# A due time for each single operation: a list scheduler's keys in a fused attention and recurrence kernel

## The chip, the cores and the metric

The kernel runs on one core of one Trainium2 chip. The metric is the device time of one execution in microseconds (us); the time before is the median of three runs. The core has five engines that each work through their own queue in order: PE (matmul), DVE (vector), ACT (scalar functions), POOL (general) and SP, which here only starts transfers. In the profile, PEld is the loading of weights into PE.

## The reference, cut to what matters

The input is x of 2 batches, 2048 rows, 256 features. A layer of gated linear attention with 16 heads comes first: each score of query t and key s is multiplied by a decay (from a running sum of gates) and by a weight that depends on the level of t XOR s. Then follow an output projection and two layer norms, a short gated recurrence over the two batches, and a last layer norm.

```python
Q = (x @ Wq.T); K = (x @ Wk.T); V = (x @ Wv.T); dl = (x @ Wdl.T)
g = -exp(A_log) * softplus(x @ Wdt.T + dt_bias);  cg = cumsum(g, axis=1)
Lam = softplus(Lp * dl)
W = (Q K^T) * S**-0.5 * exp(cg_t - cg_s) [s <= t] * Lam[t, level(t, s)]
x = layernorm(x + layernorm_g_b((W V) @ Wout.T + x))
# recurrence over the two batches, at each of the 2048 rows:
c = sigmoid(x wf + c uf + bf) * c + sigmoid(x wi + c ui + bi) * tanh(x wc + c uc + bc)
h = tanh(x wo + c_final uo + bo)
x = layernorm(x + h)
```

## The kernel before, in words

The 2048 rows are cut into 16 chunks of 128. Within a chunk, scores are computed in full; over chunks, four running states (N0 to N3, one for each bit of the chunk's number) carry the sums that later chunks need. Most matmuls are split into two half-precision parts, a high one and a low one (names ending in h and l), so that each product is three matmuls.

For every chunk, `body` calls `project` (tile pv: values and gate inputs; z, m, u, ln: softplus; pc: running sum; RP, pt, RT: rows that go to memory and come back as R and st), `keys` (pqk, with F and L as its two parts), `attend` (pu, pS: the new state; arg and DL: exponentials; sc: scores; pi: the sum over values; pin: the part from the states; YT) and `finish` (po, layer norms, gt and tg: gates, pcu, ph, hh, out). In chunk 0, the weights wo and fw are also loaded, by nine transfers through a ring of two x1 buffers, and pg (a small product with the initial state of the recurrence) is computed from them.

None of these calls starts an instruction. `Engine` and `Recorder.add` record 3845 operations; an operation is one instruction, or a group of matmuls that is kept together (918 groups stand for 10382 matmuls). `depend` finds which operation needs which. `order` then makes the final order of each engine's queue, with a small simulation: an engine that is free takes, of the operations whose inputs are ready and whose buffers are free, the one with the lowest key `late`. `issue` writes the instructions out in that order, all at one line of the code (L536 in the profile), so views by line tell nothing here and views by tile do.

The keys before: `DUE` has one due time for each chunk's output. `late` is carried back from there over the dependences (an operation must be done a duration and a latency ahead of its earliest user). Then `BIAS`, one number for each kind of operation (engine and tile, with own numbers for the first, the last and the last but one chunk: @0, @9, @8), is added. `FIRST` sets the order of the first sixteen transfers by hand. `STICK` would make PE prefer its present mode (matmuls over 128 rows, over 64 rows, or into 32 columns); it is negative, so `max(..., 0)` leaves it without effect.

`BUFS` gives the number of buffers of each ring; a ring's tiles are taken in the order in which they were recorded. `BANKS` caps how many of the eight banks that PE writes to each class of tile may hold: y (pv, pc, pt, pqk), z (po, pt_x, gt, pcu, ph), x (pu, pS, pin), a (arg), s (sc), p (pi), t (gates of the last chunk).

Of the kernel before, what the change touches and what calls it, by code (L numbers as in the profile page):

```python
# [22 lines left out]
P = 128  # L23
B, T, D = 2, 2048, 256
# [8 lines left out]
DUE = [  # L33
    2677.57, 7721.13, 18978.35, 19716.23, 26604.1, 27450.81, 30772.73, 32390.67,
    34188.43, 36425.9, 37687.87, 40156.28, 43733.31, 46896.49, 47598.73, 59076.43,
]
BIAS = {
    'DVE:id16': -544.41, 'POOL:mhalf': -2585.45, 'POOL:ones': -884.87, 'POOL:RP': 1536.59, 'DMA:xt32@0': -4046.65,
    'DVE:xth@0': 1406.88, 'POOL:xtl@0': -518.54, 'DMA:xn@0': -2368.1, 'DMA:LpB@0': -3281.08, 'POOL:LpB@0': 860.85,
    'DVE:LpB@0': -244.97, 'DMA:bc_dtb@0': -2440.29, 'DMA:stg_wv@0': -6352.72, 'ACT:wv_h@0': -1203.55,  # L40
    'DVE:wv_l@0': 268.05, 'DMA:bc_Alog@0': -6629.31, 'ACT:bc_Alog@0': -1742.76, 'DVE:bc_Alog@0': -856.29,
    'DMA:mk@0': -4013.56, 'DMA:tri@0': -3595.99, 'DMA:stg_wq@0': -3921.89, 'ACT:wq_h@0': -1587.01,
    'DVE:wq_l@0': 1004.73, 'DMA:stg_wk@0': -4796.3, 'ACT:wk_h@0': 1541.09, 'DVE:wk_l@0': 3050.85,
    'DMA:st@0': -6284.79, 'DMA:R0@0': -6277.05, 'DMA:R1@0': -5991.07, 'POOL:SH@0': 665.45, 'POOL:SL@0': -2142.9,
    'POOL:VZ0@0': 1168.73, 'POOL:VZ1@0': -2626.46, 'PE:pv@0': -2541.05, 'DVE:z@0': -3273.44, 'ACT:VZ0@0': -4024.21,
    'POOL:z@0': -405.5, 'DVE:m@0': 572.33, 'ACT:u@0': 300.83, 'ACT:ln@0': 419.02, 'DVE:u@0': -1545.81,
    'ACT:LL@0': -482.21, 'POOL:g@0': -945.72, 'POOL:gp@0': 847.34, 'POOL:gr@0': 2525.08, 'PE:pc@0': -832.96,
    'POOL:LL@0': -1927.28, 'POOL:lf@0': -892.19, 'DVE:RP@0': 1443.6, 'DVE:r1@0': -759.26, 'PE:pt@0': -4539.93,
    'ACT:RT@0': -4433.14, 'DMA:scr@0': -628.34, 'DMA:cg2@0': -2529.67, 'POOL:E@0': -1904.15, 'ACT:E@0': -1974.72,
    'POOL:wv@0': 181.98, 'PE:pqk@0': 64.39, 'ACT:F@0': 1604.82, 'DVE:L@0': 240.14, 'DMA:bc_lng@0': 2134.89,  # L50
    'DMA:bc_lnb@0': -3284.28, 'DMA:bc_bo@0': 2756.69, 'DMA:ic@0': 2678.73, 'DMA:fb@0': 1506.14,
    'DMA:stg_wo@0': 214.04, 'ACT:wo_h@0': 749.49, 'DVE:wo_l@0': 13.57, 'DMA:stg_fw@0': 1917.56,
    'ACT:fw_h@0': -4483.73, 'DVE:fw_l@0': 3214.87, 'DVE:ich@0': 420.52, 'DVE:icl@0': -4538.93, 'PE:pg@0': 1562.45,
    'DVE:gb@0': 1718.11, 'PE:pu@0': 476.98, 'ACT:Uh@0': 2949.46, 'DVE:Ul@0': 1151.14, 'PE:pS@0': 1579.04,
    'ACT:N0@0': -3364.34, 'POOL:Ne0@0': -1812.42, 'POOL:Nt0@0': 2666.57, 'PE:arg@0': 1940.26, 'ACT:DL@0': 617.53,
    'PE:sc@0': 1032.21, 'DVE:DL@0': -2154.89, 'PE:pi@0': 14.24, 'ACT:YT@0': -2007.66, 'DVE:YTl@0': -1029.9,
    'ACT:SH@0': -122.62, 'DMA:xc@0': -943.46, 'PE:po@0': 1994.93, 'DVE:o@0': 25.16, 'POOL:xc@0': 1259.58,
    'DVE:st6@0': -1858.28, 'DVE:mv@0': -3427.79, 'POOL:rs@0': -1949.61, 'DVE:x1@0': -5553.71, 'PE:pt_x@0': -1400.7,
    'ACT:tr_x@0': -2328.9, 'DVE:tr_x@0': 2309.54, 'PE:gt@0': -1288.93, 'ACT:tg@0': -946.21, 'DVE:ct@0': -235.27,
    'DVE:c20@0': -3271.11, 'ACT:chh@0': -1127.08, 'DVE:chl@0': 554.25, 'DVE:c21@0': -872.21, 'PE:pcu@0': 3059.02,  # L60
    'DVE:cu@0': 1460.37, 'PE:ph@0': 1875.67, 'DVE:hh@0': -3488.44, 'ACT:hh@0': 132.07, 'POOL:hh@0': 3054.19,
    'DMA:out@0': 3049.1, 'DMA:xt32': -1810.23, 'DVE:xth': 64.72, 'POOL:xtl': -114.25, 'DMA:xn': -34.41,
    'PE:pv': -827.63, 'DVE:z': -1783.61, 'ACT:VZ1': -2672.79, 'POOL:z': 778.86, 'DVE:m': -789.82, 'ACT:u': 160.38,
    'ACT:ln': 591.53, 'DVE:u': 565.39, 'ACT:LL': 4374.65, 'POOL:g': 743.3, 'POOL:gp': -706.56, 'POOL:gr': 1663.66,
    'PE:pc': -2010.17, 'POOL:LL': 2926.67, 'POOL:lf': 3821.96, 'DVE:RP': -662.55, 'DVE:r1': -2759.89,
    'PE:pt': -165.69, 'ACT:RT': 659.27, 'DMA:scr': -1065.41, 'DMA:cg2': -986.92, 'DMA:st': 2349.73,
    'DMA:R0': -4459.06, 'DMA:R1': -920.98, 'POOL:E': 164.31, 'ACT:E': 3751.96, 'POOL:wv': -2316.25,
    'PE:pqk': 3231.38, 'ACT:F': 2373.65, 'DVE:L': 1459.54, 'POOL:ca': 2673.82, 'ACT:coef': 777.82,
    'PE:pu': 1486.59, 'ACT:Uh': -1034.21, 'DVE:Ul': -1341.83, 'PE:pS': -1300.83, 'ACT:N1': -1363.27,
    'POOL:Ne1': 3295.45, 'POOL:Nt1': -3412.65, 'POOL:mt': -860.48, 'POOL:N1': 1496.08, 'PE:arg': 10.51,  # L70
    'ACT:DL': -378.27, 'PE:sc': 1271.55, 'DVE:DL': 214.57, 'PE:pi': -1471.85, 'PE:pin': 557.54, 'DVE:Yi': 2234.51,
    'ACT:Yh': 1604.54, 'POOL:Yl': 569.07, 'ACT:YT': -714.54, 'DVE:YTl': -122.31, 'ACT:SH': 3886.77,
    'POOL:SL': -2249.79, 'DMA:xc': 1825.76, 'PE:po': -3323.98, 'DVE:o': -660.15, 'POOL:xc': -169.22,
    'DVE:st6': -348.25, 'DVE:mv': -2225.59, 'POOL:rs': 414.73, 'DVE:x1': -228.81, 'PE:pt_x': -545.23,
    'ACT:tr_x': -194.42, 'DVE:tr_x': 94.93, 'PE:gt': -1722.42, 'ACT:tg': -1182.38, 'DVE:ct': -4965.5,
    'DVE:c20': -807.68, 'ACT:chh': -2859.38, 'DVE:chl': -3393.25, 'DVE:c21': 92.69, 'PE:pcu': -3235.88,
    'DVE:cu': 958.49, 'PE:ph': 1685.23, 'DVE:hh': -2322.3, 'ACT:hh': -1393.34, 'POOL:hh': 1020.15,
    'DMA:out': -1687.37, 'ACT:VZ0': 887.84, 'ACT:N0': -1579.9, 'POOL:Ne0': 662.46, 'POOL:Nt0': 2273.86,
    'POOL:acc0': 1222.8, 'ACT:N2': 2274.54, 'POOL:Ne2': -1305.11, 'POOL:Nt2': 3789.98, 'POOL:N2': -2988.84,
    'DVE:tq': -1338.55, 'POOL:Yi': -418.52, 'POOL:acc1': -4347.71, 'ACT:N3': -1472.76, 'POOL:Ne3': -1671.15,  # L80
    'POOL:Nt3': -1206.59, 'POOL:N3': 747.56, 'DMA:xc@8': 15056.81, 'PE:po@8': 11984.32, 'DVE:o@8': 12872.18,
    'POOL:xc@8': 12701.25, 'DVE:st6@8': 9516.16, 'DVE:mv@8': 11273.9, 'POOL:rs@8': 13415.76, 'DVE:x1@8': 7496.93,
    'PE:pt_x@8': 12669.14, 'ACT:tr_x@8': 11859.29, 'DVE:tr_x@8': 8427.28, 'PE:gt@8': 10079.09,
    'ACT:tg@8': 16255.28, 'DVE:ct@8': 13065.88, 'DVE:c20@8': 12123.56, 'ACT:chh@8': 6769.1, 'DVE:chl@8': 13861.4,
    'DVE:c21@8': 9374.46, 'PE:pcu@8': 9104.07, 'DVE:cu@8': 14670.33, 'PE:ph@8': 10197.25, 'DVE:hh@8': 14713.5,
    'ACT:hh@8': 13013.82, 'POOL:hh@8': 17906.53, 'DMA:out@8': 8066.82, 'DMA:xt32@9': -3472.99,
    'DVE:xth@9': -6943.2, 'POOL:xtl@9': -7979.66, 'PE:pv@9': -7250.49, 'DVE:z@9': -7399.69, 'ACT:VZ1@9': -5093.65,
    'POOL:z@9': -8444.59, 'DVE:m@9': -3821.67, 'ACT:u@9': -8298.34, 'ACT:ln@9': -7589.28, 'DVE:u@9': -8544.13,
    'ACT:LL@9': -4666.75, 'POOL:g@9': -6445.41, 'POOL:gp@9': -525.04, 'POOL:gr@9': 1071.48, 'PE:pc@9': -5094.17,
    'POOL:LL@9': -7512.85, 'POOL:lf@9': -7085.42, 'DVE:RP@9': -8900.61, 'DVE:r1@9': -5745.08, 'PE:pt@9': -6171.97,  # L90
    'ACT:RT@9': -9289.92, 'DMA:scr@9': -5138.62, 'DMA:cg2@9': -12451.75, 'DMA:st@9': -8335.6, 'DMA:R0@9': -4913.0,
    'DMA:R1@9': -1320.23, 'PE:pqk@9': -5086.21, 'ACT:F@9': -2346.26, 'DVE:L@9': -4425.52, 'POOL:ca@9': -1966.77,
    'POOL:acc0@9': -4203.44, 'POOL:acc1@9': -2628.34, 'POOL:acc2@9': -6977.55, 'ACT:coef@9': -5726.39,
    'PE:arg@9': -8364.73, 'ACT:DL@9': -6371.85, 'PE:sc@9': -2442.58, 'DVE:DL@9': -5936.8, 'PE:pi@9': -8104.24,
    'PE:pin@9': -6842.43, 'DVE:Yi@9': -7958.54, 'DVE:tq@9': -4871.42, 'POOL:Yi@9': -9414.91, 'ACT:Yh@9': 923.7,
    'DVE:Yl@9': -13.59, 'ACT:YT@9': -5899.02, 'DVE:YTl@9': 948.32, 'DMA:xc@9': -3131.16, 'PE:po@9': -10407.06,
    'DVE:o@9': -6391.56, 'POOL:xc@9': -5874.17, 'PE:warm@9': 2241.77, 'DVE:st6@9': -3233.97, 'DVE:mv@9': -6158.55,
    'POOL:rs@9': -4272.53, 'DVE:x1@9': -8481.89, 'PE:pt_x@9': -10891.67, 'ACT:tr_x@9': -8747.79,
    'DVE:tr_x@9': -3011.58, 'DVE:b16@9': -459.04, 'PE:ph1@9': 2189.17, 'PE:gt0@9': -1044.0, 'ACT:tg@9': -4313.81,
    'DVE:ct@9': -4064.32, 'DVE:c20@9': -8811.46, 'ACT:chh@9': -9398.28, 'DVE:chl@9': -4364.2, 'PE:gt1@9': -8791.8,  # L100
# [1027 lines left out]
```

## Time and profile before

| what | value |
|---|---|
| median of 3 runs | 614.29 us (613.6 to 614.72) |
| the profiled execution, its own time | 615.93 us |
| its span, first to last instruction | 614.1 us |
| mean granted TensorE clock | 0.991 |
| PE busy | 585.6 us, 95% |
| weight loads busy | 504.2 us, 82% |
| DVE busy | 502.4 us, 82% |
| ACT busy | 383.4 us, 62% |
| POOL busy | 303.5 us, 49% |
| transfers | 46.36 MB, mean 75 GB/s |

The profiled execution is 1.64 us longer than the median; 1.8 us of its time lie around the span. A matmul's record lasts longer than the time until the next one starts, since matmuls are pipelined: busy time on PE is the union of such records. Where this text speaks of a pitch, it means the time from one matmul's start to the next one's start.

### The profile page before, as it was taken

To read this page: it belongs to the slowest core of one execution; us is meant where nothing else is said; L and a number is where in the kernel's file an instruction comes from. 1 tells how busy PE (TensorE), PEld (TensorE's weight loads), DVE (VectorE), ACT (ScalarE), POOL (GpSimd) and SP (SyncE) were. 2 spreads that over 40 slices of the span, in tenths; PEclk is the share of its full clock that TensorE was granted. 3 is DMA by queue.
4 is the path that set the end of the run, shared out by engine and by line. 5 is a ranking of instruction groups with operands and counts; after the bars stand their busy time and mean duration, and the time that the engine had idled before them with its cause. 6 is when DMAs were issued, how large, how long until landed. Compare 5 with 4: busy or idle time off the path is not lost.

```text
span 614.1 us, 24206 instructions
## 1 busy us (share of the span) xinstructions
PE 585.6 (95%) x10382; PEld 504.2 (82%) x10382; DVE 502.4 (82%) x1196; ACT 383.4 (62%) x914; POOL 303.5 (49%) x666
## 2 busy tenths in 40 slices
PE   5988999999999999999999999999999999999894
PEld 2776788988898788978889888888988889888794
DVE  5977958888879997789786888897978879787974
ACT  4666587465784856558664674857467594664552
POOL 4461646134735729244772464547376455353432
PEclk9998999999999999999999999999999999999997
DMA  8785134311243205041411514114050512203001
GB/s 245 182 189 130 36 73 91 90 35 38 60 101 91 71 3 141 20 108 35 110 36 37 125 37 91 54 25 119 20 141 21 108 37 75 70 4 101 27 2 35
DMA packets 70139, 46.36 MB, mean 75 GB/s; under 512 B 23984, under 2 KB 67760, under 8 KB 70000
## 3 DMA queue, kind: packets, MB, share of 16 engines
q1 hardware_dynamic: 70032, 44.82, 29.3%
q8 instruction: 81, 1.33, 0.9%
q14 instruction: 26, 0.21, 0.1%
HBM read 35.63 MB, written 9.18 MB: 73 GB/s over the span
## 4 chain that ended last, share of the span: by engine, by line
PE 45%; DVE 23%; POOL 13%; ACT 9%; DMA 6%; issue 3%; SPq 0%; POOLq 0%; ACTq 0%; DVEq 0%
PE gt L536 10%; PE pqk L536 9%; PE pi L536 4%; PE sc L536 4%; POOL rs L536 3%; DVE DL L536 3%; PE ph L536 3%; DVE L L536 3%; ACT DL L536 3%; DVE m L536 3%; PE pv L536 3%; PE arg L536 2%; PE pin L536 2%; DVE st L536 2%; PE pu L536 2%
## 5 line engine op out<-in xcount | busy, mean ns | idle before, releaser
L536 PEld LDWEIGHTS <-fw_h 128*128 128x128 f16 x1176 | 90.9, 98 | 5.0 <-ACT fw_h L536 2.0
L536 ACT ACTIVATE F<-pqk 128x512 f16<-128x512 f32 x128 | 73.7, 616 | 30.3 <-PE pqk L536 28.5
L536 DVE SCALAR_TENSOR_TENSOR L<-pqk,F 128x512 f16<-128x512 f32 x128 | 82.6, 676 | 5.9 <-ACT F L536 5.9
L536 DVE SCALAR_TENSOR_TENSOR DL<-sc,DL 128x512 f32<-128x512 f32 x128 | 81.7, 677 | 4.8 <-PE sc L536 3.6
L536 PE MATMUL gt<-tr_x,fw_h 128*128 128x128 f16 x768 | 82.6, 219 | 0.3 <-DVE tr_x L536 0.2
L536 PEld LDWEIGHTS <-wk_h 128*128 128x128 f16 x992 | 69.9, 98 | 6.2 <-issue 0.6
L536 ACT ACTIVATE tg<-gt,gb 128x128 f32<-128x128 f32 x192 | 53.8, 373 | 33.9 <-PE gt L536 33.3
L536 ACT ACTIVATE DL<-arg 128x512 f32<-128x512 f32 x128 | 68.1, 616 | 6.8 <-PE arg L536 6.5
L536 PE MATMUL pqk<-xth,wq_h 128*128 128x256 f16 x256 | 70.1, 274 | 0.3 <-DVE o L536 0.3
L536 PE MATMUL gt<-tr_x,fw_l 128*128 128x128 f16 x384 | 70.0, 219 | 0.0
L536 PE MATMUL pqk<-xtl,wq_h 128*128 128x256 f16 x256 | 70.0, 273 | 0.0
L536 PE MATMUL pqk<-xth,wq_l 128*128 128x256 f16 x256 | 69.9, 273 | 0.0
L536 PEld LDWEIGHTS <-F 64*128 64x128 f16 x2048 | 60.8, 93 | 10.9 <-issue 8.4
L536 PE MATMUL pqk<-xth,wk_l 128*128 128x256 f16 x256 | 69.8, 272 | 0.0
L536 PE MATMUL pqk<-xth,wk_h 128*128 128x256 f16 x256 | 69.8, 272 | 0.0
L536 PE MATMUL pqk<-xtl,wk_h 128*128 128x256 f16 x256 | 69.7, 272 | 0.0
L536 PEld LDWEIGHTS <-fw_l 128*128 128x128 f16 x588 | 57.3, 98 | 1.8 <-DVE fw_l L536 1.0
L536 PEld LDWEIGHTS <-wq_h 128*128 128x128 f16 x512 | 48.6, 98 | 8.0 <-issue 0.7
L536 POOL TENSOR_TENSOR Yi<-Yi,tq 128x256 f32<-128x256 f32 x32 | 25.3, 791 | 49.2 <-DVE Yi L536 33.3
L536 PEld LDWEIGHTS <-wk_l 128*128 128x128 f16 x496 | 46.2, 98 | 4.1 <-issue 1.0
L536 PE MATMUL sc<-F 64*128 64x128 f16 x512 | 46.4, 218 | 0.3 <-DVE L L536 0.3
L536 PEld LDWEIGHTS <-L 64*128 64x128 f16 x1024 | 45.2, 93 | 0.7 <-issue 0.4
(179 smaller groups left out, 1809.7 us busy)
## 6 DMA issues: line engine op xcount, KB each, us to landing
st<-cg SPq DMA_DIRECT2D x16, 768.0 KB, 6.3
xt<-xT SPq DMA_DIRECT2D x16, 256.0 KB, 2.8
xc<-x SPq DMA_DIRECT2D x16, 256.0 KB, 2.8
scr<-RT SPq DMA_DIRECT2D x16, 256.0 KB, 2.9
R<-scr SPq DMA_DIRECT2D x32, 128.0 KB, 2.9
xn<-x SPq DMA_DIRECT2D x15, 256.0 KB, 3.2
out<-hh SPq DMA_DIRECT2D x15, 256.0 KB, 2.2
stg_fw<-fw SPq DMA_DIRECT2D x8, 256.0 KB, 3.7
```

The costliest lines, as they stand in the source:

```text
L536: getattr(eng.real, meth)(*[real(x) for x in a], **{q: real(x) for q, x in k.items()})
```

## The change

The keys of all 3845 operations now stand in one table, two characters for each operation, in the order of recording. `DIGITS` are 89 printable characters; the number of a pair is read in base 89, and 200 is taken away. `order` no longer carries due times back over the dependences, and `DUE`, `BIAS`, `FIRST` with its field `rank`, and the term with `STICK` are gone. The ring sizes `BUFS` and the caps `BANKS` have other values. What is computed, the recorded operations, their dependences, the model of durations and latencies, and the rule by which a free engine chooses are as before.

```diff
-DUE = [
-    2677.57, 7721.13, 18978.35, 19716.23, 26604.1, 27450.81, 30772.73, 32390.67,
...
-BIAS = {
-    'DVE:id16': -544.41, 'POOL:mhalf': -2585.45, 'POOL:ones': -884.87, 'POOL:RP': 1536.59, 'DMA:xt32@0': -4046.65,
...
+DIGITS = "".join(chr(c) for c in range(33, 127) if chr(c) not in "\"\\'{}")
+PLAN = (
+    "_A#+Y4#U#y$)#d$NSU$3#x$2$G$/3g,/$-<YFn$x&C$3&uR5$2R^,[%D$2-U$,Zs$*%dFy0w$*$4$)$,$$!y$/]W$(E`JzOWZq#t$4,T0K!&#y+~"
...
+BUFS = {
+    'xt32': 1, 'xth': 2, 'xtl': 2, 'xn': 1, 'L': 3, 'F': 3, 'z': 1, 'm': 2, 'u': 2, 'ln': 1, 'LL': 1, 'g': 8,
+    'gp': 1, 'gr': 8, 'lf': 3, 'r1': 1, 'RT': 1, 'scr': 2, 'cg2': 2, 'E': 1, 'wv': 1, 'x1': 2, 'Uh': 2, 'Ul': 3,
+    'DL': 2, 'YT': 2, 'YTl': 4, 'xc': 1, 'o': 1, 'st6': 3, 'mv': 3, 'rs': 2, 'tr_x': 3, 'tg': 1, 'ct': 4, 'c20': 2,
+    'chh': 6, 'chl': 3, 'c21': 1, 'cu': 1, 'hh': 2, 'ca': 1, 'coef': 3, 'mt': 1, 'Yi': 5, 'Yh': 1, 'Yl': 5,
+    'acc0': 3, 'tq': 1, 'acc1': 1, 'acc2': 1, 'st69': 4, 'mv9': 2, 'rs9': 3,
 }
-BUFS = {
-    'xt32': 1, 'xth': 2, 'xtl': 2, 'xn': 1, 'L': 3, 'F': 3, 'z': 1, 'm': 1, 'u': 1, 'ln': 3, 'LL': 1, 'g': 3,
-    'gp': 10, 'gr': 3, 'lf': 4, 'r1': 1, 'RT': 1, 'scr': 2, 'cg2': 3, 'E': 1, 'wv': 1, 'x1': 2, 'Uh': 1, 'Ul': 5,
-    'DL': 2, 'YT': 4, 'YTl': 3, 'xc': 1, 'o': 1, 'st6': 4, 'mv': 4, 'rs': 3, 'tr_x': 2, 'tg': 1, 'ct': 1, 'c20': 1,
-    'chh': 2, 'chl': 6, 'c21': 1, 'cu': 4, 'hh': 2, 'ca': 3, 'coef': 2, 'mt': 1, 'Yi': 2, 'Yh': 1, 'Yl': 1,
-    'acc0': 5, 'tq': 1, 'acc1': 1, 'acc2': 1, 'st69': 7, 'mv9': 5, 'rs9': 2,
-}
-BANKS = {'y': 8, 'z': 8, 'x': 4, 'a': 7, 's': 5, 'p': 6, 't': 7,}
-
-FIRST = ["xt32", "stg_wv", "stg_wq", "LpB", "bc_dtb", "stg_wk", "bc_Alog", "tri", "mk", "xt32", "stg_wq", "stg_wk", "st", "R0", "R1", "xn"]
+BANKS = {'y': 6, 'z': 6, 'x': 8, 'a': 6, 's': 6, 'p': 8, 't': 3,}
 MERGE, WARM, TABLE, MODE = 0.6, 0.37, 1.28, 0.1
...
-    def order(self, outs):
+    def order(self, code):
...
-        late = [1e9] * n
-        for i in range(n - 1, -1, -1):
-            late[i] = min([outs.get(i, 1e9)] + [late[s] - ops[i].dur - ops[i].lat for s in succ[i]])
-        bias = BIAS
-        late = [x + bias.get(o.kind, bias.get(o.kind.split("@")[0], 0.0)) for x, o in zip(late, ops)]
-        late = [o.rank - 1e6 if o.rank >= 0 else x for x, o in zip(late, ops)]
-        stick = max(bias.get("STICK", 0.0), 0.0)
+        base = len(DIGITS)
+        late = [DIGITS.index(code[2 * i]) * base + DIGITS.index(code[2 * i + 1]) - 200 for i in range(n)]
...
-                    m = min((k for k in range(3) if ready[e][k]), key=lambda k: ready[e][k][0][0] + (stick if e == "PE" and k != mode else 0))
+                    m = min((k for k in range(3) if ready[e][k]), key=lambda k: ready[e][k][0][0])
```

## The prediction

> **What bounds the kernel now.** I read the page first, then the busy time by stretches, then what PE waited for, then the chain of waits, and last the transfers' queue at the start. The page, and PE's waits:
>
> ```profile
> span 614.1 us, 24206 instructions
> PE 585.6 (95%) x10382; PEld 504.2 (82%) x10382; DVE 502.4 (82%) x1196; ACT 383.4 (62%) x914; POOL 303.5 (49%) x666
> ...
> PE pv L536 <- DVE xth L536: 5.9, 1, 5.9
> PE arg L536 <- DVE L L536: 2.3, 6, 0.8
> PE pg L536 <- ACT fw_h L536: 1.8, 1, 1.8
> PE ph L536 <- ACT chh L536: 1.6, 1, 1.6
> PE pv L536 <- POOL xtl L536: 1.6, 1, 1.6
> ```
>
> PE is the bound. The waits are in us in total, times, longest: the first and the fifth are the head of the kernel, the fourth is its tail, and all others together come to about 12 us. The stretches show where PE idles (length, then busy us of PE, PEld, DVE, ACT, POOL, then the granted clock):
>
> ```profile
> 40.00:60.00 20.00, 15.61 (x291) 11.66 (x293) 13.25 (x28) 10.43 (x26) 7.23 (x16) 0.91 0.71 158
> 100.00:200.00 100.00, 99.83 (x1797) 86.82 (x1795) 84.54 (x207) 61.51 (x150) 44.71 (x92) 1.00 0.30 73
> 200.00:300.00 100.00, 97.58 (x1788) 84.21 (x1786) 87.88 (x207) 66.00 (x156) 52.16 (x116) 1.00 0.28 71
> 560.00:580.00 20.00, 18.04 (x408) 15.03 (x408) 18.63 (x47) 10.93 (x23) 6.36 (x10) 1.00 0.37 98
> ```
>
> The reader sees an ordinary stretch (100 to 200: 0.2 us idle) and two poor ones: 4.4 us idle at 40 to 60, where the clock is granted at 0.91 too, and 2.0 us at 560 to 580.
>
> Busy time hides how much of this is streaming. The chain has runs of one kind of matmul, from which pitches follow:
>
> ```profile
> 68.70 1.19 PE pv L536 x6
> 75.37 1.01 PE pi L536 x32
> 99.69 3.97 PE pqk L536 x36
> 113.93 1.29 PE pin L536 x96
> 115.22 1.36 PE sc L536 x48
> 499.79 2.01 PE gt L536 x36
> ```
>
> That is 198, 32, 110, 13.4, 28.3 and 56 ns. The values used next are taken over all starts in the trace, within 5% of these. Counts by pitch: pqk 1536 x 109 = 167.4; gt 1728 x 56 = 96.8; sc 1536 x 28.2 = 43.3; pv 192 x 196 = 37.6; pi 1024 x 30.5 and 128 x 56 = 38.4; arg 1024 x 29 = 29.7; pu 120 x 216 = 25.9; ph 207 x 109 = 22.6; pS 20.9; po 20.9; pin 1536 x 13.5 = 20.7; the seven small ones (pcu, pt, pt_x, warm, pc, pg and rounding) 30.1. Sum **554.3 us**. So the span is 5.9 (before the first matmul) + 554.3 + 47.5 (lost between starts) + 6.4 (after the last start). Of the 47.5, 19.7 us stand at 163 changes of mode (128 rows, 64 rows, 32 columns; 0.12 us each). By place, the loss is 7.3 us in 40 to 60, 4.2 in 560 to 580, 4.5 in the first 20 us (half of it slow first matmuls), 12.9 in 200 to 400 and about 0.8 in an ordinary 20 us.
>
> A page weighs in here. The Trainium skill, "Perfetto Trace Analysis", section "Identifying the Most-Contended Engine", says that matmul busy share is no measure of headroom and that the share of weight loads is one: its 82% would leave 110 us, and busy 95% leaves 28.5. The pitches leave 47.5, and the forecast goes by them.
>
> **The change part by part.** No instruction is added or taken away: 10382 matmuls, 1196 DVE, 914 ACT and 666 POOL instructions keep their durations. So the 554.3 us stand, and only the order, rings and banks can move the other 59.8.
>
> *The keys on PE.* Before, all operations of one kind shared a bias, so one late group could not be moved without its 15 sisters. Now it can. The poor stretches hold single events of that sort:
>
> ```profile
> 44.20 0.61 PE L536 MATMUL pt<-idb,RP 128*128 128x128 bf16 x8 [0.21 <-DVE L L536]
> 46.62 0.18 PE L536 MATMUL pg<-ich,fw_h 128*128 128x1 f16 x1 [1.82 <-ACT fw_h L536]
> 47.35 0.19 PE L536 MATMUL pg<-ich,fw_l 128*128 128x1 f16 x1 [0.55 <-DVE fw_l L536]
> ```
>
> The 24 groups of pg wait 2.7 us for fw, and pv of the next chunk is queued behind them, since PE goes in order. In 560 to 580, pS waits 1.2 us for Ul, which DVE did after layer-norm pieces; pin waits 0.6 for SL. If all three places came to the ordinary level, that would be 7.3 − 1.1 = 6.2, 4.2 − 1.0 = 3.2, and 12.9 − 10 x 0.8 = 4.9: 14.3 us. I take half, **7.1 us** (3.1 + 1.6 + 2.4). Why half: order can move other matmuls into a hole, but not make the operand earlier. The fw pieces that pg wants come by transfers that last up to 9.5 us through two x1 buffers, and that ring keeps its size. What is late next there is xth of chunk 2 (its cast starts at 48.48), so pv can't fill the hole unless DVE casts earlier too.
>
> *Changes of mode.* The term that could hold PE in its mode was without effect before, so its removal costs 0. The table is no help by itself: groups sorted by the table alone change mode 234 times, sorted by the old keys 89 times, and 163 times in the trace, since readiness breaks any sorting. Bounds: 71 more changes cost 8.5 us, 74 fewer give 8.9. I take 0, because readiness, not the key, set the 163.
>
> *The cold stretch.* In 46 to 52 the granted clock is 0.72 and 0.71, after 43 to 46 with 1.6 of 3.0 us busy; a granted 0.91 over 20 us is 1.8 us. These are inside the 7.3 above. The Trainium skill, "TensorE: Matmul & The Clock Gate", section "Part 1: The HAM clock gate", tells of an activity window of about 3.4 us with half rate after an idle one. By that rule, a new hole of about one window would cost a further 1.7 us after itself, which speaks against a table that opens one. The trace shows the one slow stretch in the middle of the kernel.
>
> *The first transfers.* The hand-made order goes. Sorting the transfers that need nothing by the table, and keeping the rings' order, gives xt32, bc_Alog, stg_wv, ic, LpB, stg_wq, stg_wk, bc_dtb, mk, stg_wq, stg_wk, stg_wo and so on. The queue before:
>
> ```profile
> 0.72 0.44 SPq L536 DMA_DIRECT2D xt<-xT  x1
> 1.23 0.45 SPq L536 DMA_DIRECT2D stg_wv<-wv  x1
> 1.71 0.47 SPq L536 DMA_DIRECT2D stg_wq<-wq  x1
> ```
>
> Each issue costs about 0.48 us of SP's queue. stg_wv is now behind one more: 0.5 us; wv_h then ends at 6.3, not 5.82, and the first matmul slips by 0.4, which PE's wait for xtl (1.6 us, from 6.46 to 8.04) covers. stg_wq is behind three more: 1.4 us; wq_l then ends at 12.1 instead of 10.72, and pqk starts at 12.27: covered by 0.1. With that cover gone, each further issue costs 0.5. ic, scattered in pieces of 4 bytes, took 5.7 us from issue to landing at 19.8. As the fourth transfer it can cost 0 to 5.7 us; I take 0, nearest to LpB and bc_dtb, which sat in the same places and delayed nothing that the waits show.
>
> *Rings and banks.* m, u, Yi, Yl, ct, chh, g and gr grow; ln, gp, Ul, cu, YT, st6 and mv shrink; x, p and s get more banks, y, z, a and t fewer, out of the same eight. In PE's waits none of the small ring users stands with over 0.7 us. Bounds: the 12 us of waits, either way; I take 0, since the waits named are for operands (L, fw, Ul, xth), not for room.
>
> *Head and tail.* 5.9 and 6.4 us are chains: xt, cast, first pv; and chh, ph, tanh, layer norm, out. No key shortens them: 0.
>
> **The sum.** The profiled execution would take 615.93 − 7.1 = 608.8. It lies 1.64 above the median of the runs shown, so against the median: 614.29 − 7.1 = **607.2 us**.
>
> **The rivals.** About 0.2%, 1.2 us, is what a measurement of this kernel can tell from no change.
>
> *A: the forecast*, 601 to 613. 601 is nearly all 14.3 us recovered.
>
> *A': more*, below 601: the 14.3 and over ten changes of mode fewer. For it: 19.7 us stand there. Against: the sorting above. Place it at 599.
>
> *B: nothing to see*, 613.1 to 615.5, taken as 614.3: PE takes what is ready, so the keys decide little; a hole that is filled comes back where the filling matmul is missing. For it: 18 of the 31 stretches of 20 us already lose at most 1.2 us each.
>
> *C: slower, by PE's queue in fixed order.* The old keys were carried back over dependences, so a producer was mostly due ahead of its user. In the table, of 3998 dependences on a PE group 1360 have the user due no later than the group, against 786 before, 73% more. A group that ends late, or stands ahead of an operand that is later on the chip than the planner thought, stalls all behind it. Place: PE's queue in the middle chunks. Price: 0.38 us for each (2.3 us in 6 waits of arg for L). If waits grow with the reversals, 12 x 0.73 = 8.8 us: 614.3 + 8.8 = 623.1, if nothing is won. It decides from about 19 new waits on (7.1 / 0.38). Against it: for DVE's products, for which PE waits most, the reversals rise only from 1373 to 1566 of 3895; and DVE is only 82% busy.
>
> *That the change does not do what it says* can be left aside for PE: its ranks by old keys and by the table correlate at 0.83, so many orders must change. For POOL (0.37) and the transfers (0.25), they change more, but POOL is busy 49%.
>
> **How the numbers follow.** A 0.64, A' 0.08, B 0.08, C 0.20. The likeliest is A with 607.2. The range 601 to 620 leaves out A' (0.08) and the half of C above 620 (0.10); 620 also holds the transfers' 5.7 us with nothing won. A's own range is 601 to 613. Faster is A and A', 0.72; same is B, 0.08; slower is C, 0.20.
>
> **What would show it.** PE's idle time in 40 to 60 falls from 4.4 to about 2 and the clock there rises above 0.91; pg no longer waits 1.8 us; 560 to 580 has over 18.5 us busy; the waits for L fall below 2.3 us. The changes of mode stay within 20 of 163. The first pqk starts at 12.3 ± 0.5. I am wrong if the loss between starts in 100 to 540 grows (C), if the start slips by over 1 us (the transfers), or if the changes of mode move by more than 30.

## The result, and the profile after

| | before | after |
|---|---|---|
| median, range (4 runs each) | 614.44 us, 613.6 to 614.72 | 619.48 us, 618.17 to 620.91 |
| after : before | | 1.0074 [1.0048, 1.0099] |
| the profiled execution, its span | 615.93, 614.1 us | 620.91, 619.1 us |
| first matmul, first pqk, after the last start | 5.89, 12.27, 6.42 us | 7.27, 14.64, 6.40 us |
| lost between starts of matmuls | 47.5 us | 51.1 us |
| of it at changes of mode | 19.7 us, 163 | 17.7 us, 147 |

The change makes the kernel 0.7% slower, where 1.2% faster was forecast: rival C's side. The sum of the pitches is the same 554.3 us, so the spans differ by 1.4 us of head and 3.6 us of loss between starts. From the page of after, its span and its busy times:

```profile
span 619.1 us, 24222 instructions
...
PE 583.1 (94%) x10382; PEld 503.9 (81%) x10382; DVE 505.0 (82%) x1196; ACT 386.1 (62%) x914; POOL 309.0 (50%) x666
```

As many instructions of each engine as before, and nearly the same busy times: only the time in which PE waits has grown. What PE waited for in after (us in total, times, longest):

```profile
PE pv L526 <- ACT wv_h L526: 7.3, 1, 7.3
PE pt_x L526 <- DVE x L526: 3.2, 5, 1.5
PE arg L526 <- DVE L L526: 2.9, 3, 1.1
PE pv L526 <- DVE wv_l L526: 2.8, 1, 2.8
PE pqk L526 <- ACT tg L526: 1.8, 1, 1.8
PE pi L526 <- issue: 1.5, 1, 1.5
```

The reader sees that the waits of before for pg (1.8) and xtl (1.6) are gone, and that new ones stand in their place: wv_l at the start, x and L in the middle, one wait of pqk for tg. pqk doesn't read tg. tg reads the bank that pqk is to write to, so this one is a wait for room. By stretches (length, busy us of PE, PEld, DVE, ACT, POOL, granted clock):

```profile
40.00:60.00 20.00, 16.55 (x353) 13.57 (x351) 16.39 (x31) 12.21 (x30) 6.41 (x13) 1.00 0.74 175
60.00:80.00 20.00, 19.64 (x409) 16.14 (x410) 17.01 (x39) 11.10 (x31) 11.39 (x30) 0.91 0.10 29
100.00:200.00 100.00, 97.47 (x1833) 85.50 (x1832) 80.80 (x196) 63.21 (x151) 46.06 (x92) 1.00 0.27 68
200.00:300.00 100.00, 96.06 (x1716) 82.08 (x1715) 84.25 (x207) 64.11 (x153) 52.53 (x117) 1.00 0.25 66
400.00:500.00 100.00, 97.27 (x1730) 83.89 (x1728) 80.21 (x194) 63.85 (x152) 53.42 (x116) 1.00 0.27 67
560.00:580.00 20.00, 18.36 (x343) 16.06 (x340) 16.41 (x48) 10.42 (x24) 8.73 (x13) 1.00 0.44 111
```

The two poor places of before (40 to 60, 560 to 580) became better by 0.9 and 0.3 us of PE's busy time. The ordinary stretches became worse: 100 to 200 from 99.83 to 97.47, 200 to 300 from 97.58 to 96.06, 400 to 500 from 99.31 to 97.27. The last of them in before:

```profile
400.00:500.00 100.00, 99.31 (x1742) 86.74 (x1740) 83.68 (x208) 65.90 (x157) 56.45 (x125) 1.00 0.30 72
```

To place the 5 us in time, I take the time at a point less the sum of the pitches of all matmuls started until then (us behind an ideal PE):

| at | 20 | 40 | 60 | 80 | 100 | 200 | 300 | 400 | 500 | 580 | 600 |
|---|---|---|---|---|---|---|---|---|---|---|---|
| before | 10.3 | 11.6 | 19.1 | 20.6 | 21.7 | 25.3 | 32.4 | 38.3 | 42.9 | 50.1 | 51.0 |
| after | 12.2 | 14.7 | 19.4 | 22.4 | 23.0 | 29.1 | 37.5 | 43.0 | 49.8 | 55.9 | 56.9 |

After is 1.9 us late at 20 and 3.1 at 40, has nearly caught up at 60 (0.3), and then loses in the middle: 1.3 late at 100, 6.9 at 500. The last 100 us give 1 us back, and the end another 0.9.

**The start.** SP's queue in after:

```profile
0.72 0.44 SPq L526 DMA_DIRECT2D xt<-xT  x1
1.22 0.44 SPq L526 DMA_DIRECT2D bc_Alog<-Alog  x1
1.70 0.43 SPq L526 DMA_DIRECT2D stg_wv<-wv  x1
2.18 0.47 SPq L526 DMA_DIRECT2D ic<-ic  x1
2.69 0.47 SPq L526 DMA_DIRECT2D LpB<-Lp  x1
3.20 0.43 SPq L526 DMA_DIRECT2D stg_wq<-wq  x1
```

and DVE's queue in the same time, with the idle time before an instruction and what ended it in brackets:

```profile
9.64 0.27 DVE L526 TENSOR_SCALAR LpB<-LpB 128x208 f32<-128x208 f32 x1 [2.15 <-DMA LpB<-Lp]
9.82 1.12 DVE L526 SCALAR_TENSOR_TENSOR wv_l<-stg_wv,wv_h 128x928 f16<-128x928 f32 x1
12.09 1.23 DVE L526 SCALAR_TENSOR_TENSOR wq_l<-stg_wq,wq_h 128x1024 f16<-128x1024 f32 x1 [1.15 <-ACT wq_h L526]
```

The same two operations before:

```profile
5.85 1.13 DVE L536 SCALAR_TENSOR_TENSOR wv_l<-stg_wv,wv_h 128x928 f16<-128x928 f32 x1
8.83 0.27 DVE L536 TENSOR_SCALAR LpB<-LpB 128x208 f32<-128x208 f32 x1 [1.86 <-DMA LpB<-Lp]
```

LpB lands late in either kernel (6.9 us from issue to use here, 6.6 before). What is new is that its scaling stands ahead of wv_l in DVE's queue. Now wv_l, which PE needs for its third matmul, waits for a transfer that it has nothing to do with. wq, issued 1.5 us later, is cast 2.6 us later (wq_h at 11.00, before 8.40). The first matmul needs wv_h: its transfer was issued 0.47 us later than before, but its cast began 1.40 us later (6.24 against 4.84). What made that transfer slower isn't shown.

**The middle.** Of PE's waits of over 0.4 us in 100 to 500, before has three (0.82, 0.58 and 0.49; 1.9 us together), after has eight, 7.4 us together: pt_x for x 1.51, 0.71 and 0.42, pqk for tg 1.79, arg for L 1.05 and 0.84, pi for Yl 0.62, pS for Ul 0.48. The loss in this time is 26.8 us (49.8 − 23.0) against 21.2, 5.6 more, and the eight waits account for 5.5 of it. The longest:

```profile
493.52 0.27 PE L526 MATMUL pqk<-xth,wq_h 128*128 128x256 f16 x1 [1.79 <-ACT tg L526]
```

**The plan beside the chip.** The simulation in `order` (the planner) keeps the start that it expects of every operation (`self.timed`). In the plan of after, LpB's scaling begins at 5.12 us and wv_l at 5.76; the chip began them at 9.64 and 9.82. Before the five groups of the middle that waited longest (0.71 to 1.79 us), the plan has PE idle for 0.00 us; so it has before two of the three waits of the kernel before. At 500 us the chip is 29.7 us behind the plan in after and 18.0 us in before (at 20 us 3.7 and 1.8).

### The profile page after: what moved, and what is told of

Read it like the earlier page. It is cut to its first block, busy times and chain, and to the rows that moved or that the text cites. A ratio compares the mean times of both kernels' runs of the same rounds, so it can differ in the third digit from the quotient of the medians.

```text
span 619.1 us, 24222 instructions
## 1 busy us (share of the span) xinstructions
PE 583.1 (94%) x10382; PEld 503.9 (81%) x10382; DVE 505.0 (82%) x1196; ACT 386.1 (62%) x914; POOL 309.0 (50%) x666
## 4 chain that ended last, share of the span: by engine, by line
PE 37%; DVE 17%; POOL 15%; ACT 7%; issue 5%; DMA 1%; SPq 0%; POOLq 0%; ACTq 0%; DVEq 0%
PE gt L526 9%; PE pqk L526 8%; POOL rs L526 4%; PE sc L526 3%; PE pi L526 3%; PE pv L526 2%; DVE DL L526 2%; PE ph L526 2%; PE pS L526 2%; DVE L L526 2%; PE arg L526 2%; DVE st L526 2%; DVE o L526 2%; ACT tg L526 2%; PE pin L526 1%
## 5 line engine op out<-in xcount | busy, mean ns | idle before, releaser
L526 ACT ACTIVATE F<-pqk 128x512 f16<-128x512 f32 x128 | 75.7, 602 | 33.3 <-PE pqk L526 32.0
L526 DVE SCALAR_TENSOR_TENSOR L<-pqk,F 128x512 f16<-128x512 f32 x128 | 85.2, 678 | 10.6 <-ACT F L526 8.2
L526 DVE SCALAR_TENSOR_TENSOR DL<-sc,DL 128x512 f32<-128x512 f32 x128 | 83.3, 679 | 6.7 <-PE sc L526 4.1
L526 ACT ACTIVATE tg<-gt,gb 128x128 f32<-128x128 f32 x192 | 56.4, 371 | 36.1 <-PE gt L526 35.5
L526 ACT ACTIVATE DL<-arg 128x512 f32<-128x512 f32 x128 | 71.1, 612 | 12.0 <-PE arg L526 11.8
L526 PEld LDWEIGHTS <-wk_h 128*128 128x128 f16 x992 | 71.2, 98 | 7.7 <-issue 0.8
L526 PE MATMUL arg<-R,st 128*128 128x64 bf16 x1024 | 41.2, 193 | 5.5 <-DVE L L526 2.9
```

What stands on the lines that cost most here:

```text
L526: getattr(eng.real, meth)(*[real(x) for x in a], **{q: real(x) for q, x in k.items()})
```

## The experiments

The theory after the first look: two causes, the start and PE's queue in the middle. Rivals: the start alone carries the loss into all chunks; the new rings and banks do it; the engines or transfers are slower through contention.

The first edits are made after the planner: its order is taken, single operations are moved within their own engine's queue, and the owners of each ring's buffers keep their turns. The line at which all instructions are issued shifts a little by that. Times are medians, ratios are to the kernel before on the same chip (614.6 to 615.9 us there), with a 95% interval. Where two such ratios are compared, as those of after and e7, both intervals count: about 2 us to either side.

### e1: after, with the first transfers of before

```diff
+START = [5, 13, 21, 9, 12, 24, 16, 20, 19, 27, 30, 283, 33, 34, 35, 8, 122, 209, 126, 125, 129, 121, 124, 123, 512]
+    queue["DMA"][:25] = START
+    behind(queue["ACT"], 17, 42)
+    behind(queue["DVE"], 11, 15)
...
```

The 25 first transfers stand in the order of before. `behind(row, x, y)` puts x right after y: the scaling of LpB (11) goes after wv_l (15), and the small casts of bc_Alog and ic go later.

> The changed kernel, with only the start put back: the first 25 transfers in the order of before, and the small operations on A_log, Lp and in_c on ACT and DVE behind the weights' conversions, as before. All later orders stay as changed. Theory 1 (the table's order fits the planner's durations, and the loss comes as many small waits of PE all along the middle): the first pqk goes from 14.6 back to about 12.3 us, but the trace of the change is only 0.4 us behind before at 60 us, so the end gains 0 to 1.5 us: 618 to 619.5. Rival 2 (the start carries the loss): 614 to 615. Rival 3 (rings and banks): 619.5, as the change.

Measured: 624.15 us, 1.0129 [1.0092, 1.0165]. The first pqk starts at 11.31, but at 40 us the kernel is 18.1 us behind, 3.4 more than after. DVE in this run:

```profile
23.89 0.69 DVE L552 SCALAR_TENSOR_TENSOR wo_l<-stg_wo,wo_h 128x512 f16<-128x512 f32 x1 [3.48 <-ACT wo_h L552]
```

My edit moved the transfers of wo back, while the rest of the order wants wo early: DVE stood 3.5 us. The same fault as in the change itself (transfers and casts in orders that don't fit), made by me. As a test of the start it is spoilt; e7 mends it.

### e2: before, with the start of after

```diff
+START = [5, 16, 13, 124, 9, 21, 24, 12, 19, 27, 30, 283, 126, 129, 33, 20, 125, 35, 209, 122, 34, 121, 8, 123, 512]
+    queue["DMA"][:25] = START
+    behind(queue["DVE"], 11, 154)
...
```

The reverse: the transfers stand in after's order (xt, bc_Alog, wv, ic, LpB and so on), and the scaling of LpB (11) and the casts of ic ahead of wv_l.

> The kernel before, with only the start of the change: its first 25 transfers and the small operations of the start in the changed order. Theory 1: 614.4 to 616, since the wait for the fw pieces at 40 to 50 us takes up most of 2.4 us. Rival 2: about 619. Rival 3: 614.4.

Measured: 616.83 us, 1.0019 [1.0003, 1.0036]. The first pqk starts at 14.09, 1.8 us late, and of it 1.2 us (0.0019 x 615; 0.2 to 2.2 by the interval) are left at the end. So the start costs about a quarter of the 0.74% in the old order. It isn't the whole loss.

### e3: after, with ic moved back

```diff
+    behind(queue["DMA"], 124, 121)
+    behind(queue["DVE"], 153, 291)
+    behind(queue["DVE"], 154, 153)
```

> The changed kernel, with the transfer of ic (pieces of 4 bytes) moved from the fourth place to behind bc_lng, and the two casts of ic on DVE behind the conversions that they stood ahead of. If ic in front is what delays the weights: stg_wq lands 1 us or more earlier than at 11.0, and pqk starts at 13 to 13.6 instead of 14.6. If the order of the others and the scaling of Lp ahead of wv_l carry the delay: pqk starts at 14.2 or later. End of kernel by theory 1: 618.5 to 619.5; by rival 2: 616 to 618.

Measured: 621.62 us, 1.0095 [1.0069, 1.0122]: nothing won. The first pqk is at 14.08 still, since LpB's scaling still stands ahead of wv_l and DVE waits 3.58 us for it there. ic, which I had given up to 5.7 us, isn't the delay.

### e7: after, with half of the start

```diff
+START = [5, 13, 21, 9, 12, 24, 16, 19, 27, 30, 283, 126, 129, 124]
+    queue["DMA"][:14] = START
+    behind(queue["DVE"], 11, 15)
...
```

Only 14 transfers change place: the first eleven go as before does them (without tri), wo (126) and fw (129) stay early as after wants them, and ic (124) comes last. The casts are moved as in e1.

> The changed kernel with only the first eleven transfers (x, the weights of the first chunk and their small companions) in the order of before; wo and fw keep their early place, ic comes behind them; the small operations on A_log, Lp and in_c go behind the conversions as in the first experiment, which had wo late and lost 3.5 us on DVE for that. Theory 1: pqk starts at about 12 us and the end gains 1 to 2 us, as the kernel before lost 1.2 by the new start: 617.5 to 618.5. Rival 2 (start carries the whole): 614 to 615. If the wait for fw takes it up: 619 to 620.

Measured: 617.55 us, 1.0037 [1.0018, 1.0057]; the first pqk at 11.78. Against after, 0.37% or 2.3 us are won. All eight waits of the middle are still there, of the same sizes within 0.03 us (1.80 for tg, 1.49 for x, 1.06 and 0.83 for L): they don't come from the late start.

### e8: after, with 16 moves in PE's queue

```diff
+MOVES = [
+    ("PE", 713, 714), ("PE", 905, 906), ("PE", 243, 242), ("PE", 349, 345), ("PE", 135, 128), ("PE", 239, 236),
...
+        queue[e].insert(b, queue[e].pop(a))
```

Sixteen of the 918 groups of matmuls change place, by up to ten places; nothing else does. They were chosen on a replay of the trace: each queue in order, each instruction with its measured length, starting when its operands and its room are there, and a move kept where the end came earlier.

> The changed kernel with 16 moves on PE's queue alone, picked by the same replay, in which it falls from 620.3 to 618.0. If PE's own order were at fault (a late group ahead of ready ones), these moves would win back about 5 us: 614 to 615. Theory 1 with the loss mostly in the queues that feed PE: 617 to 619.5.

Measured: 616.62 us, 1.0021 [1.0005, 1.0036], 3.3 us less than after. From PE's waits in this run:

```profile
PE pv L552 <- DVE wv_l L552: 2.5, 1, 2.5
PE pt_x L552 <- DVE x L552: 2.5, 4, 1.5
PE arg L552 <- DVE L L552: 1.2, 2, 0.8
PE pqk L552 <- ACT tg L552: 1.2, 1, 1.2
```

The start is as late as in after. Of the eight waits of the middle seven are left, 5.5 us for 7.4: L is shorter (1.2 for 1.9) and so is tg (1.2 for 1.8), and one of 0.71 for x is gone. By the table of time behind, 3.7 us are won by 80 us (18.7 against 22.4), 2.1 more by 500, and 1.8 are given back in 500 to 580. In both the 3.7 and the 1.8, 1.7 us are one stretch of slow clock (3.4 us at half rate): the trace of after has it at 62 us, this one at 574. So PE's order alone can win these 3.3 us in after. Whether sixteen such moves would win as much in before was not tried.

### e11: both repairs

```diff
+    queue["DMA"][:14] = START
...
+    for e, a, b in MOVES:
+        queue[e].insert(b, queue[e].pop(a))
```

e7's start and e8's sixteen moves in one kernel.

> The changed kernel with both repairs that won something alone: the first eleven transfers in the order of before (2.3 us won against the change) and the 16 moves on PE (3.3 us won). If the loss is the sum of a slow start and of waits in PE's queue: 5 us or more below the change, at the kernel before or below, 612 to 615. If both repairs win the same time twice: 616 to 617.

Measured: 614.7 us, 0.9984 [0.9964, 1.0004]. The time is that of before again: 1.0074 less 0.0037 less 0.0053 is 0.9984, so the two gains add up. That does not make them the two causes of the loss. By the time behind, e11 stands at 19.6 at 100 and at 43.8 at 500: it loses 24.2 us in the middle, where after loses 26.8 and before 21.2. So 3.0 of the 5.6 us are still lost there, and they are made up outside it: at 100 us e11 is 2.1 us ahead of before.

### e5 and e6: moves on four engines, in both kernels

```diff
+MOVES = [
+    ("DVE", 803, 805), ("POOL", 368, 373), ("DVE", 1185, 1188), ("DVE", 879, 880), ("DVE", 680, 687), ("POOL", 411, 417),
+    ("DVE", 492, 495), ("POOL", 474, 477), ("ACT", 443, 436), ("DVE", 497, 507), ("PE", 383, 387), ("DVE", 594, 593),
...
```

80 moves in after (e5) and 73 in before (e6, the first of them shown), chosen as in e8; 13 of them on ACT in each.

> The changed kernel with 80 operations (37 on DVE, 15 on PE, 15 on POOL, 13 on ACT) put up to ten places earlier or later in their own queues, tables and rings as changed. The moves were picked by a replay of the trace of the change: every queue in its order, every operation with the length that the trace shows, every wait for the operations it depends on; the replay falls from 620.3 to 608.6 with them. Theory 1 (the order is fitted to durations that the chip does not have): most of it is real, 609 to 614, 1 to 2% below the change. Rival 4 (contention: the engines run slower under the new order, whatever the order of details): 617 to 621, no gain.

> The same for the kernel before: 73 moves (25 on DVE, 20 on PE, 15 on POOL, 13 on ACT), picked by a replay of its own trace, in which it falls from 614.9 to 604.9. Theory 1: 605 to 610, 1 to 1.6% below before, and so faster than both kernels. Rival 4 or a replay that is itself fitted too closely: 613 to 617.

Measured: e5 616.11 us, 1.0019 [1.0001, 1.0036]; e6 616.18 us, 1.0015 [0.9996, 1.0034]. e5 won 3.4 us on after, about what PE's moves alone had won. e6 gained nothing on before, and the groups by line show something that the replay had missed. ACT's table loads in before (instructions, busy us, mean ns):

```profile
L536 ACT ACT_TABLE_LOAD x14 | 18.0, 1283 | 0.1
L532 ACT ACT_TABLE_LOAD x13 | 16.7, 1283 | 0.2
```

The same two groups in e6:

```profile
L562 ACT ACT_TABLE_LOAD x17 | 21.8, 1283 | 0.2
L558 ACT ACT_TABLE_LOAD x16 | 20.5, 1283 | 0.3
```

An activation that passes one of another function adds loads of tables: six more, 6 x 1.283 = 7.7 us in ACT's queue, and PE then waits for ACT (arg, 2.17 us at 301). My choice of moves had not counted them.

### e9 and e10: the same without ACT

```diff
+MOVES = [
+    ("PE", 634, 635), ("POOL", 395, 397), ("PE", 300, 299), ("POOL", 366, 372), ("POOL", 471, 479), ("POOL", 504, 503),
+    ("PE", 575, 576), ("POOL", 411, 418), ("DVE", 493, 492), ("POOL", 506, 514), ("DVE", 150, 146), ("POOL", 163, 170),
...
```

69 moves in before (e9, the first of them shown: 26 on PE, 21 on DVE, 22 on POOL) and 86 in after (e10: 21, 42, 23); ACT's order is kept.

> The kernel before with 69 moves on PE, DVE and POOL (26, 21, 22), ACT's queue left as it was. The run before it of this kind also moved 13 operations on ACT, which split runs of tanh and made 34 loads of function tables out of 28, 7.7 us that the replay did not count. With ACT kept, the replay falls from 614.9 to 605.3. Theory 1: 606 to 611. If replays cannot be trusted at all: 614 to 617.

> The changed kernel with 86 moves on PE, DVE and POOL (21, 42, 23), ACT's queue and the start as changed. The replay falls from 620.3 to 608.4. Theory 1: 609 to 614, below the 616.1 with moves on ACT too. If the loss sits in ACT's order or in contention: 616 to 620.

Measured: e9 **607.46 us, 0.9864 [0.9836, 0.9892]**; e10 612.98 us, 0.9966 [0.9943, 0.9990]. e9 beats both kernels, with the keys, rings and banks of before. Its stretches:

```profile
40.00:60.00 20.00, 16.42 (x357) 12.81 (x354) 13.99 (x30) 11.67 (x29) 8.07 (x19) 0.91 0.69 153
200.00:300.00 100.00, 98.95 (x1826) 85.64 (x1823) 88.92 (x210) 68.22 (x166) 55.62 (x129) 1.00 0.30 72
560.00:580.00 20.00, 19.32 (x484) 16.54 (x484) 18.54 (x54) 10.79 (x26) 8.42 (x13) 1.00 0.20 55
```

At the three places of the prediction PE is busy 0.8, 1.4 and 1.3 us longer than before, and the middle has no wait of over 0.4 us left. The engines' busy times are nearly those of before (PE 583.0, DVE 502.3, ACT 383.5 us), so contention isn't what separates these kernels; order alone is worth some 8 us here (6.6 to 10.1 by the interval).

### e14: after, with e10's moves and e7's start

```diff
+    queue["DMA"][:14] = START
...
+    for e, a, b in MOVES:
+        queue[e].insert(b, queue[e].pop(a))
```

> The kernel after with both repairs: the 86 moves in the queues of PE, DVE and POOL (612.98 us by themselves) and the first transfers and casts in the order of before, with wo and fw kept early (617.55 us by themselves, 2.3 us won against the kernel after). Theory 1 (the start and the queues behind it are two separate losses, which add): 612.98 less about 2.3 is 610 to 611.5 us. Theory 2 (the moves were fitted to the late start, so an earlier start runs into other waits): 612.5 to 615 us. Theory 3 (the rest is what rings and banks of the change cost, which neither touches): at least 3 us above the 607.46 of the kernel before with its 69 moves; 610.5 or more is in line with it, 608 or less refutes it.

Measured: 611.43 us, 0.9951 [0.9933, 0.9968], 1.5 us under e10 (0.9 by the ratios). The third theory fits, and the first by its number only, since 2.3 us were to be won. It stays 4 us above e9 (5.3 by the ratios, which allow for the different chips), lost little by little between 80 and 400 (19.6 to 38.0 us behind, e9 19.1 to 32.2). So moves on measured lengths (in after with the start mended too) win about 8 us in either kernel, and the distance between the two is no smaller than at first (0.74%, 4.6 us). Whether rings and banks keep it, or an order that moves by up to ten places don't mend, isn't settled.

### e4 and e15: keys and rings in the wrong pairing

```diff
-BANKS = {'y': 6, 'z': 6, 'x': 8, 'a': 6, 's': 6, 'p': 8, 't': 3,}
+BANKS = {'y': 8, 'z': 8, 'x': 4, 'a': 7, 's': 5, 'p': 6, 't': 7,}
...
```

Only `BUFS` and `BANKS` are exchanged (the diff is e4's); the planner makes the order again. e4 is the table with the rings and banks of before, e15 the keys of before with those of after.

> The changed table, with the rings and banks of before; the planner makes its order anew with them. Rival 3 (rings and banks carry the loss): back to about 614, or lower. Theory 1: the table is tied to every detail of the planner's simulation, so another set of rings breaks it: far slower, 650 to 710; the planner's own count for this order is 672, against 585 for the changed kernel and 593 for the kernel before.

> The kernel before with the ring sizes and caps of banks of the kernel after and nothing else of the change, the order made again: the fourth of the four pairings of keys with rings. Both kernels have one pairing each (614.4 and 619.5 us), and the table with the rings and caps of before took 697.6 us, 78 more than with its own. Theory 1 (rings and keys belong together on either side, but an order by kinds with due times carried back loses less in a wrong pairing than a table of single keys): the planner's own count is 627.7 us, 35 above that of before; on the chip 640 to 660 us, a loss of 26 to 46. Theory 2 (the new rings and caps are worse by themselves, whatever the keys, and the table makes up for it): the loss is as large as that of the table in the wrong pairing, 680 us or more. Theory 3 (the new rings and caps are better or indifferent by themselves): 620 us or less.

### e12 and e13: 0.01 us more on each latency

```diff
-    LAT = dict(PE=0.2, ACT=0.15, DVE=0.13, POOL=0.08, DMA=0.95)
+    LAT = dict(PE=0.21, ACT=0.16, DVE=0.14, POOL=0.09, DMA=0.96)
```

These are numbers of the planner's model alone; nothing on the chip changes but the order. e12 is after with it, e13 before.

> The changed kernel, with 0.01 us added to each of the five latencies by which the planner thinks; it makes its order anew. No hardware number changes, only what the planner believes, by less than the differences between one execution and the next. Theory 1 (table fitted to the planner's exact numbers): far slower, 670 to 710; the planner's own count goes from 585 to 678. If the table orders the work by something that the chip shares: 617 to 625.

> The kernel before, with 0.01 us added to every latency that the planner reckons with, and the order made again from the keys of before. The same edit on the kernel after took 706.5 us, 91 more than the kernel before. Theory 1 (a table of single keys is fitted to the planner's exact numbers, keys by kind that are carried back over the dependences much less): the order falls apart far less, the planner's own count grows by 29 us only (593 to 622), and the chip shows 630 to 655 us. Theory 2 (both orders are fitted to the numbers alike, and the table is no more brittle): the loss is like that of the table, 690 us or more. Theory 3 (the order of before does not depend on the exact numbers at all): 613 to 620 us.

Measured, with the planner's own count of the span beside each:

| | keys of before | table |
|---|---|---|
| own rings | 614.4 us (planner 592.6) | 619.5 us (585.1) |
| the other's rings | e15 644.28, 1.0455 [1.0387, 1.0523] (627.7) | e4 697.62, 1.1348 [1.1308, 1.1388] (672.2) |
| latencies + 0.01 us | e13 642.10, 1.0462 [1.0431, 1.0494] (622.0) | e12 706.54, 1.1456 [1.1406, 1.1506] (677.7) |

Three things follow. By its own count the planner thinks the table 7.5 us faster (585.1 against 592.6), and the chip says 5 us slower. A hundredth of a microsecond in the model costs the table 87 us and the keys of before 28: both sets of keys are fitted to the exact numbers, the table three times as closely. And with a model or rings for which neither was fitted, the table is the worse of the two by 53 to 64 us. The keys of before lose 29 us with the rings of after, and the table 78 with those of before, so neither set of rings can be judged without its keys.

Two limits go with this. What these four runs change is the order that the planner makes, and its own count rises nearly as the time does: 92.6, 87.1, 29.4 and 35.1 us for 87, 78, 28 and 29 on the chip (e12, e4, e13, e15). They show how brittle the keys are in the making of an order; how much a finished order loses when the chip's lengths differ from the planned ones they don't show. And part of each loss is slow clock: one less the granted clock, times the span, is some 33 us on the mean of e12's runs and 32 of e4's, 12 and 13 of e13's and e15's, against 3 to 5 in the two kernels with their own rings.

## Why the prediction was wrong

**Which step failed.** The step "forecast by half of three places, with nothing lost elsewhere". Its working took the poor places of before as room to win and the ordinary stretches as given.

- *40 to 60, 3.1 us expected*: 2.3 came (the loss there fell from 7.3 to 5.0), and PE's idle time fell to 3.45, not to 2. pg (two groups, 36 matmuls; the prediction's 24 groups are a misreading) no longer waits. The granted clock rose to 1.00 there, but the slow clock only moved: 0.91 in 60 to 80.
- *560 to 580, 1.6 expected*: 1.1 came (4.2 to 3.1). Busy 18.36, not over 18.5.
- *200 to 400, 2.4 expected*: the loss grew by 0.8 instead (12.9 to 13.7).
- *Elsewhere, 0 expected*: 2.7 lost in 100 to 200, 2.2 in 400 to 500, 1.2 in 60 to 80, 1.3 in the first 40 us and 1.4 ahead of the first matmul. This is the term that turned the sign: in 100 to 500 as a whole 5.6 us more were lost, 5.5 of them in eight waits of PE. I had said which observation would prove me wrong (a growing loss in 100 to 540), and it came.

**The first transfers**, costed at 0: wrong, and I looked in the wrong queue. I followed each transfer to its cast and found covers of 0.4 and 0.1 us, but I followed SP's queue alone. The larger part of the cost sits in DVE's: LpB's scaling ahead of wv_l. The first pqk came at 14.64 instead of 12.3, which is 2.4 us at the start; 1.2 of it are left at the end in the old order (e2), 2.3 are won by mending it in the new one (e7). Range and condition were stated right ("the start slips by over 1 us"), the suspect (ic) was wrong (e3).

**Rings and banks**, 0: not settled. The reason, that no wait is for room, failed: one is (1.79 us of pqk for tg). In a wrong pairing they cost 29 to 78 us (e15, e4), and what stays between e9 and e14 may be theirs. They can't be costed apart from the keys.

**Changes of mode**, 0 and within 20 of 163: 147 came, 2.0 us less. Right in kind; a small gain that I had not taken.

**Head and tail**, 0: the tail held (6.40), the head didn't (1.4 us).

**Half and the size of what can be won**: 14.3 us at three places, half of it by order. e9 won 7.9 us in the kernel before, and with no more than a change of order. So that much was there to be won; that this table would win it was assumed.

**Rival C** was right in side and place. Its mechanism, a group that stands ahead of an operand later on the chip than planned, is seen in five of the waits, where the plan has none; that reversed keys make such waits isn't shown. It was dearer per wait than I had it. I took 0.38 us for each and a need of 19 new waits; there are five more waits of over 0.4 us in 100 to 500, 0.9 us each (7.4 / 8). Its 8.8 us were in truth 5.6. It got 0.20 because the reversals of DVE's products rose little. The 73% was the wrong count as well: it is of what others need from PE. Of the 5304 dependences of PE's groups on what they need, the keys reverse 2118 before and 2244 after, 6% more. Counting reversals doesn't tell how much slack an order leaves.

What is shown: the loss stands in the start and in waits of PE in the middle, with busy times nearly as before; the start costs 1.2 to 2.3 us (e2, e7); at the start and at the five longest waits of the middle, the chip departs from the plan. What isn't shown is that PE's order is what the change spoiled: moves win as much in before, and leave the distance as it was (e9, e14). What rings and banks have to do with it was not separated from the keys. That the table fails because it is fitted to the planner's numbers is argued, from the plan's own times and from e12, e13, e4 and e15. No run gave the planner the chip's own lengths and made a new table.

## What to carry to other kernels

An order that is fitted operation by operation to a model of time can promise a gain that is smaller than the model's error: here the planner was within 9 us of the chip for losses of 28 to 87 us, and had the sign of a 7.5 us gain wrong. Before trusting such a gain, move the model by a hundredth of a microsecond and see whether the plan holds, and lay the planned starts beside a trace. When first transfers are reordered, follow the queue of the engine that consumes them, not only the one that issues them: one small scaling that waits for a late transfer holds up all that is queued behind it. And where the order itself is the lever, choose moves on measured lengths: 69 such moves beat both orders here.

## What the runs showed of the hardware that was not expected

PE can stand still with nothing awaited. In after, PE goes on at 60.36 after 1.45 us for which the trace names no cause but the issue of instructions:

```profile
60.36 0.85 PE L526 MATMUL pi<-DL,VZ 128*32 128x128 f32 x19 [1.45 <-issue]
```

The queue of code in 57.5 to 59 us (packets, MB, share of 16 engines):

```profile
q8 instruction: 1, 0.02, 5.6%
```

The page of after counts 81 such packets in the whole kernel:

```profile
q1 hardware_dynamic: 70032, 44.82, 29.0%
q8 instruction: 81, 1.33, 0.9%
```

That is 16.4 KB each, and 20764 matmuls and weight loads over 81 are 256 instructions each. In after the packet ended at 58.91 and PE went on 1.45 us later. The pause comes at the same place in PE's queue, within two instructions, in e1, e3, e5, e8, e11 and e14 (0.59 to 1.97 us), at one other instruction in e10 and e14 (1.55 and 1.57 us), and once in e13 (0.61 us). Each time PE goes on 1.2 to 1.6 us after such a packet has ended. So PE seems to wait for its code; that was seen and not tested. Not every kernel with that order has the pause: e7 has none of over 0.5 us. The Trainium skill, "Runtime: NRT & Kernel Launch", section "Instruction fetch mechanics", has code come in blocks of 16 KiB, 256 instructions, at a cost that is mostly hidden. The block's size agrees with these packets. If the pause is that cost, 1.45 us of it were not hidden, at one of 81 packets.

The clock: it was slow once in the middle in either kernel. In after:

```profile
58.00:60.00 2.00, 0.91 (x33) 0.64 (x21) 2.00 (x6) 0.77 (x3) 0.00 (x0) 1.00 0.02 3
60.00:62.00 2.00, 1.64 (x69) 1.41 (x70) 0.15 (x2) 0.76 (x3) 0.00 (x0) 1.00 0.03 8
62.00:64.00 2.00, 2.00 (x12) 1.42 (x11) 1.78 (x5) 1.20 (x3) 0.67 (x1) 0.56 0.00 0
64.00:66.00 2.00, 2.00 (x44) 1.99 (x43) 1.75 (x4) 1.01 (x2) 0.98 (x1) 0.59 0.00 0
66.00:68.00 2.00, 2.00 (x74) 1.95 (x72) 1.74 (x4) 2.00 (x6) 1.29 (x4) 1.00 0.04 8
```

Here the cost of a hole falls after it, when PE is busy again: some 3.4 us at half rate ((0.44 + 0.41) x 2 / 0.5), which is 1.7 us lost. It does not follow every hole: in e11 PE is busy 0.29 of the 2 us at 56 to 58, and the clock stays at 1.00 in all of 56 to 66. The section on the clock gate that the prediction names gives one window of about 3.4 us at half rate, and this trace agrees. A table of busy time doesn't show it, since PE is 100% busy there.
